# Score products of the next unit moved between two groups of transposes in the attention loop of a hybrid block

## The chip, the cores and the metric

The kernel runs on one core of one Trainium2 chip. The metric is the device time of one execution in microseconds; lower is better. A core has five engines that run at the same time: TensorE (matrix products; PE in the profile, with its weight loads shown apart as PEld), VectorE (DVE), ScalarE (ACT), GpSimd (POOL) and SyncE (SP), which here issues most of the transfers. TensorE writes its results to PSUM, a small memory of eight banks, from which VectorE or ScalarE must copy them before a bank can be used again.

## What is computed

The reference is a chain of four residual blocks over `x` of shape 4 x 256 x 512: an attention with rotary embedding, 32 heads of width 16 and an adapter prefix of 10 tokens; a gated linear layer; a state-space mixer on an inner width of 8192; and the same gated linear layer again. The change touches the attention alone:

```python
x = x + attn(_layernorm(x), ...)      # the change is in here
x = x + ffn(_layernorm(x), ...)
x = x + mixer(_layernorm(x), ...)
x = x + ffn(_layernorm(x), ...)

# attn, per batch b (4 of them), T = 256, 32 heads of width 16
q, k = rope(q), rope(k)
scores = einsum('bhqd,bhkd->bhqk', q, k) / sqrt(16)   # causal mask
y = einsum('bhqk,bhkd->bhqd', softmax(scores), v)
a = gating[0] * softmax(einsum('bhqd,xhkd->bhqk', q, ak) / sqrt(512))
y = y + einsum('bhqk,xhkd->bhqd', a, av)
return einsum('btc,oc->bto', y, w_proj)
```

## The kernel before

The attention is done in 32 units, unit `i` being four heads of batch `b = i // 8` (`u = i % 8`). A loop over `i` issues one pass for each unit; work of several units is in flight in each pass, one stage apart. In this loop the order of TensorE's instructions is exactly that of the program text (the loop stands in a manual schedule for TensorE), while VectorE, ScalarE and GpSimd get an order from the scheduler of the framework when the program is built. Every engine then runs its own instructions in that fixed order, and an instruction that has to wait holds up all that stand behind it on its engine. TensorE's instructions in pass `i` are, in this order:

- `scores(b, u)`: 16 products of queries and keys (`sc`, the code's line 492) into four banks of the pool `ps_s`, which only the scores use. The keys are needed a second time with neighbouring rows swapped; the swap is a pair of transfers on SP (`pc<-pc`, line 348) that follows ScalarE's copy of the transposed keys (`pc<-trp`, line 447).
- on even `u`, `adapter_scores`: products `pa` (line 457), which ScalarE copies out as `sa` (line 462);
- `pieces`: four transposes `trp` (line 444) of queries or keys for a later unit;
- a "long" step, where one is due: 12 products of 128x512 that make queries, keys, values or an output projection (`pq`, `po`, `pd`; lines 115 to 117);
- `weigh`: the values weighted by the exponentials of unit `i - 2` (`py`, lines 533 and 539);
- `turn`: 12 transposes of the exponentials of unit `i - 1` in three groups of four (`ptr`, line 523), each group into a bank of its own. ScalarE copies the first and third group, VectorE the second (`eT`, line 524);
- `gathered`: two transposes of the weighted values of unit `i - 3` (`try`, line 553), from which VectorE makes the reciprocal `ry` of the row sums and the result `y` (lines 558 and 559);
- on even `u`, the transposes `tra` (line 466) of the adapter scores, which ScalarE copies to `as` (line 467); and, in some passes, the transposes of a "turn" step: `tr` of a normalised tile (line 166), `try2` of finished results (line 610), `pt` of the adapter's weights (line 584).

All of these but `sc` and `py` take their banks from one pool, `ps` (tag `m`), which has three banks. Banks are given out when the program is built, and the first write into a bank waits for the last reader of what was in it before.

VectorE and ScalarE turn scores into exponentials. For each of the four heads VectorE adds the causal mask and takes the row maximum in one custom instruction (line 500, `e<-sc`, `nmx`): four over 256 columns and four over 128 columns. ScalarE then takes the exponentials (line 508), again four wide and four narrow ones. Unit `i`'s exponentials are needed by `turn` in pass `i + 1`.

`scores` is a generator, and where the pass resumes it decides what is issued there. Its steps in the kernel before: products and row maxima up to the first `yield`, wide exponentials up to the second, narrow ones up to the third. The pass used it so:

```python
scoring = scores(b, u)
next(scoring)          # products, row maxima
...                    # pa, trp
next(scoring)          # wide exponentials
...                    # long step, py, ptr
next(scoring)          # narrow exponentials
```

After the attention come the two gated layers and the mixer, whose products (lines 115 to 117, `pp`, `pog`, and line 1252) fill the rest of the time.

Of the kernel before, what the change touches and what calls it, by code (L numbers as in the profile page):

```python
# [79 lines left out]
def hybrid_kernel(  # L80
# [191 lines left out]
    def attention(later, region):  # L272
        with ExitStack() as es:
# [19 lines left out]
            def weights(w, src, tag, engine, pool=p2):  # L293
                for k in range(0, KC, 2):
                    r = pool.tile([P, 2, C], F32, name="ar", tag=tag)
                    if pool is p1:
                        load(r, src[:, k : k + 2, :])
                    for j in range(2):
                        if pool is not p1:
                            load(r[:, j, :], src[:, k + j, :])  # L300
                        split([v[:, k + j, :] for v in w], r[:, j, :], engine)
# [171 lines left out]
            def begin(b):  # L473
                state[b] = {
                    "as": p1.tile([P, 2, NH, NA], F32, name="as"),
                    "y": p1.tile([P, 2, C], F32, name="y"),
                    "ya": p1.tile([P, 2, C], F32, name="ya", tag="ya"),
                    "yT": [p1.tile([P, KC, L], F32R, name=f"yT{j}") for j in range(2)],
                }

            def scores(b, u):

                qT, kT = turned_[b, u // 2]
                es_ = [p2.tile([P, 4, (c + 1) * P], F32, name=f"e{c}", tag=f"e{c}") for c in range(2)]
                tops = {}
                banks_ = [ps_s.tile([P, 3, P], F32, name="sc", tag="sc") for _ in range(4)]
                for c, at in ((1, slice(0, 2)), (0, slice(2, 3))):
                    n = (c + 1) * P
                    for v in range(2):
                        for r in range(4):  # L490
                            rows = slice(32 * r, 32 * r + 32)
                            nc.tensor.matmul(
                                banks_[r][:, at, :].rearrange("p k i -> p (k i)"),
                                qT[rows, 0, u % 2, c * P : (c + 1) * P], kT[rows, v, u % 2, :n],
                                start=(v == 0), stop=(v == 1),
                            )
                for c, at in ((1, slice(0, 2)), (0, slice(2, 3))):
                    tops[c] = nm = p3.tile([P, 4], F32, name="nmx", tag="nmx", bufs=4)
                    for r in range(4):
                        nc.vector.tensor_tensor_reduce(  # L500
                            es_[c][:, r, :].rearrange("p (k i) -> p k i", i=P), banks_[r][:, at, :],
                            mask[:, 1 - c :, :], -1.0, 3e38, ALU.add, ALU.min, nm[:, r : r + 1],
                        )

                yield
                for c in (1, 0):
                    for r in range(4):
                        nc.scalar.activation(  # L508
                            es_[c][:, r, :], es_[c][:, r, :], AF.Exp, scale=-1.0, bias=tops[c][:, r : r + 1],
                        )  # L510
                    if c == 0:
                        all_es[8 * b + u] = es_
                    yield
# [31 lines left out]
            def taken(py):  # L545
                ys = p2.tile([P, L], F32, name="ys")
                nc.vector.tensor_copy(ys, py)
                return ys
# [87 lines left out]
            def fed(f, t):  # L636
                yield "turn", None
                xs = normed(f.norm, t)
                yield "long", max(0, B * 8 + t - 2)
                f.tile(t, xs, [ps.tile([P, FH], F32, name="pd", tag="m") for _ in range(2)])  # L640
# [35 lines left out]
            n = B * 8  # L676
# [5 lines left out]
            def moved(j, i):  # L682

                v = next(j, None)
                if v is None:
                    nexts.pop(j, None)
                else:
                    nexts[j] = v[0], i + 1 if v[1] is None else v[1]

            def step(stage, i):  # L690

                for j in [j for j, (s, r) in nexts.items() if s == stage and r <= i]:
                    moved(j, i)
# [15 lines left out]
            with tc.manual_schedule(engines={nc.tensor.engine}):  # L709
                for i in range(n):  # L710
                    b, u = divmod(i, 8)
                    if u == 0:
                        if i:
                            begin(b)
                        if b + 1 < B:
                            moved(prepared(b + 1), i)
                    scoring = scores(b, u)
                    next(scoring)
                    if i in FEEDS:
                        moved(fed(feed, FEEDS[i]), i - 1)  # L720
                    if i == 2:
                        nc.scalar.activation(a_s, a_s, AF.Exp)
                        nc.gpsimd.tensor_scalar(a_s, a_s, -1.0, None, ALU.mult)
                    if i == 3:
                        weights(wp_s, wproj, "ya", nc.gpsimd, p1)
                    if u % 2 == 0 and i > 0:
                        asides.append(adapter_scores(b, u // 2))
                        next(asides[-1])
                    if part:
                        next(part)  # L730
                    part = None
                    next(scoring)
                    step("long", i)
                    step("values", i)
                    if 2 <= i:
                        py = weigh(*divmod(i - 2, 8), eTs.pop(i - 2))
                    if 1 <= i:
                        eTs[i - 1] = turn(all_es.pop(i - 1))
                    next(scoring)
                    if 2 <= i:  # L740
                        yss[i - 2] = taken(py)
                    if 3 <= i:
                        gathered(*divmod(i - 3, 8), yss.pop(i - 3))
                    while asides:
                        next(asides.pop(0), 0)
                    step("turn", i)
                    if u == 7:
                        moved(adapted(b), i)
                    if 3 <= i:
                        if (i - 3) % 8 == 6:  # L750
                            moved(closed((i - 3) // 8, (0, 1, 2)), i)
                        if (i - 3) % 8 == 7:
                            moved(closed((i - 3) // 8, (3,)), i)

                    b, u = divmod(i + 3, 8)
                    if b < B:
                        part = pieces(b, u // 2, (i + 1) % 2)
                        next(part)
                    if i == 23:
                        inner.close()  # L760
                        feed = Feed("f", *(
                            later.enter_context(
                                tc.tile_pool(name=f"f{v}", bufs=v, side="right", reuse_waits="tile")
                            ) for v in (1, 2)
                        ))
                    if i in range(23, 27):
                        feed.weights(i - 23, nc.gpsimd)
                        feed.norm.stats(i - 23)
                    if i == 26:
                        feed.norm.root(0, 4)  # L770


                b = B - 1
                step("long", n)
                yss[n - 2] = taken(weigh(b, 6, eTs.pop(n - 2)))
                eTs[n - 1] = turn(all_es.pop(n - 1))
                gathered(b, 5, yss.pop(n - 3))
                step("turn", n)
                moved(fed(feed, 3), n - 1)
                step("turn", n)  # L780
                step("long", n + 1)
                step("values", n + 1)
                yss[n - 1] = taken(weigh(b, 7, eTs.pop(n - 1)))
                gathered(b, 6, yss.pop(n - 2))
                moved(closed(b, (0, 1, 2)), n)
                moved(fed(feed, 4), n)
                step("turn", n + 1)
                gathered(b, 7, yss.pop(n - 1))
                moved(closed(b, (3,)), n)
                step("long", n + 2)  # L790
                step("turn", n + 2)
                xs5 = normed(feed.norm, 5)
                assert not nexts, nexts
# [1118 lines left out]
```

## Time and profile before

| what | value |
|---|---|
| median of 3 runs | 1804.76 us (1802.36 to 1805.3) |
| profiled execution, its own time | 1805.61 us |
| its span | 1803.8 us |
| TensorE busy, weight loads | 1745.7 us (97%), 1417.8 us (79%) |
| VectorE, ScalarE, GpSimd busy | 1427.7 us, 1268.7 us, 240.9 us |
| mean granted TensorE clock | 0.989 |
| first and last score product | 31.7 us, 281.0 us from the span's start |
| first and last transpose of exponentials | 44.1 us, 298.0 us |

The profile is that of one execution. Its span runs from the first to the last instruction that it records; the execution's own time is 1.8 us longer. Busy times are sums over an engine's instructions. The ends of matmuls are modelled, so that PE shows as busy more than it works; starts of matmuls and of weight loads, and what a wait was ended by, are what the reading rests on. In a row of the timeline the columns are start and duration in microseconds, engine, code line, operation, output and inputs, sizes, how often, and in brackets the idle time before and what ended it.

### The profile page before, as it was taken

Reading aid. Unit: us, or ns where it says so; the run is one execution under the profiler, and the core shown is the slowest. Engines: PE = TensorE matmul, PEld = TensorE weight load, DVE = VectorE, ACT = ScalarE, POOL = GpSimd, SP = SyncE. Lnnn points to the kernel's source line nnn. Section 1 sums busy time; section 2 is a strip of 40 time slices with the busy share of each in tenths; the row PEclk is TensorE's granted clock in tenths of the full one; section 3 lists DMA queues with packets and bytes.
Section 4 is the critical chain, followed back from the end, with each engine's and each line's share of the span. In section 5 each row is a group of like instructions: output and inputs, shape, how many; then the busy total and the mean of one; then the engine's idle time right before and its main releaser. Section 6 shows DMA issues by size and latency. Waiting matters only on the chain.

```text
span 1803.8 us, 33220 instructions
## 1 busy us (share of the span) xinstructions
PE 1745.7 (97%) x12862; PEld 1417.8 (79%) x12862; DVE 1427.7 (79%) x2523; ACT 1268.7 (70%) x2293; POOL 240.9 (13%) x249
## 2 busy tenths in 40 slices
PE   7999988899999999999999999999999999999998
PEld 6777767778877888888888888888888888888877
DVE  5676676889998788787878797878788878887777
ACT  5676684578887668766866686668667867777754
POOL 5332320111110111011110101110111101101100
PEclk8999999999999999999999999999999999999999
DMA  4000100122344234423433252325333433343231
GB/s 157 19 19 19 47 26 26 43 71 99 109 127 137 80 106 154 120 85 99 153 100 100 88 162 90 109 81 176 103 94 112 135 106 94 115 138 115 85 97 56
DMA packets 136941, 173.71 MB, mean 96 GB/s; under 512 B 12752, under 2 KB 78032, under 8 KB 136784
## 3 DMA queue, kind: packets, MB, share of 16 engines
q1 hardware_dynamic: 127712, 138.57, 25.5%
q10 hardware_dynamic: 9072, 33.03, 4.8%
q8 instruction: 101, 1.65, 0.4%
q14 instruction: 56, 0.46, 0.1%
HBM read 131.71 MB, written 35.65 MB: 93 GB/s over the span
## 4 chain that ended last, share of the span: by engine, by line
PE 76%; DVE 11%; ACT 8%; issue 3%; DMA 1%; POOL 1%; SPq 0%; ACTq 0%; DVEq 0%; POOLq 0%
PE pp L115 13%; PE pp L117 12%; PE pp L116 12%; PE pyy L1252 7%; PE pog L115 6%; PE pog L117 6%; PE pog L116 6%; PE trx L1233 3%; DVE acc L980 2%; ACT e L508 1%; ACT em L1213 1%; DVE em L1226 1%; PE pq L115 1%; PE ptr L523 1%; PE pq L117 1%
## 5 line engine op out<-in xcount | busy, mean ns | idle before, releaser
L115 PE MATMUL pp<-mx,w 128*128 128x512 f32 x1144 | 459.3, 401 | 0.0
L117 PE MATMUL pp<-mx,w 128*128 128x512 f32 x1144 | 446.8, 391 | 0.0
L116 PE MATMUL pp<-mx,w 128*128 128x512 f32 x1144 | 446.1, 390 | 0.0
L1285 POOL TENSOR_TENSOR sq<-sq,x 128x1024 f32<-128x1024 f32 x54 | 132.1, 2446 | 1177.7 <-ACT x L1284 1177.7
L117 PEld LDWEIGHTS pp<-mx,w 128*128 128x128 f32 x1144 | 214.7, 188 | 46.2
L115 PEld LDWEIGHTS pp<-mx,w 128*128 128x128 f32 x1144 | 214.8, 188 | 44.7
L980 DVE SCALAR_TENSOR_TENSOR acc<-pp,cw_s,acc 128x1012 f32<-128x1012 f32 (+2 forms) x192 | 244.5, 1274 | 4.3
L116 PEld LDWEIGHTS pp<-mx,w 128*128 128x128 f32 x1144 | 215.1, 188 | 40.5
L1226 DVE TENSOR_TENSOR em<-em,gm 128x1280 f32<-128x1280 f32 x128 | 189.5, 1489 | 72.1 <-ACT em L1221 72.1
L115 PE MATMUL pog<-wo,gh 128*128 128x512 f32 x512 | 201.2, 393 | 2.0 <-DVE x L1381 2.0
L117 PE MATMUL pog<-wo,gh 128*128 128x512 f32 x512 | 200.2, 391 | 0.9 <-DVE gh L1364 0.9
L116 PE MATMUL pog<-wo,gh 128*128 128x512 f32 x512 | 199.8, 390 | 0.0
L1236 DVE TENSOR_TENSOR xd<-trx,dt_t 128x512 f32<-128x512 f32 x128 | 82.4, 685 | 141.5 <-PE trx L1233 141.5
L1152 ACT ACT_TABLE_LOAD x63 | 80.8, 1283 | 139.1 <-DVE acc L980 138.9
L1443 ACT ACTIVATE gt<-pp 128x1024 f32<-128x1024 f32 x64 | 65.6, 1025 | 145.0 <-PE pp L117 145.0
L1252 PEld LDWEIGHTS pyy<-em,xd 64*64 64x64 f32 x4096 | 130.2, 133 | 44.2 <-issue 17.6
L1213 ACT ACTIVATE em<-r,end_t 128x128 f32<-128x128 f32 x512 | 163.1, 389 | 0.8
L1252 PE MATMUL pyy<-em,xd 64*64 64x256 f32 (+3 forms) x4096 | 157.8, 300 | 3.1 <-DVE em L1226 3.0
L115 PEld LDWEIGHTS pog<-wo,gh 128*128 128x128 f32 x512 | 96.3, 188 | 24.8 <-issue 2.8
L508 ACT ACTIVATE e<-e,nmx 128x256 f32<-128x256 f32 (+1 forms) x256 | 97.2, 448 | 24.3 <-DVE nmx L500 24.2
L117 PEld LDWEIGHTS pog<-wo,gh 128*128 128x128 f32 x512 | 96.4, 188 | 22.3 <-DVE gh L1364 2.1
L116 PEld LDWEIGHTS pog<-wo,gh 128*128 128x128 f32 x512 | 96.4, 188 | 19.5
(324 smaller groups left out, 3094.5 us busy)
## 6 DMA issues: line engine op xcount, KB each, us to landing
wr<-in_win_dram SPq DMA_DIRECT2D x144, 256.0 KB, 2.7
r<-cumd SPq DMA_DIRECT2D x256, 128.0 KB, 2.9
spill<-gb ACTq DMA_DIRECT2D x63, 512.0 KB, 2.8
gr<-spill SPq DMA_DIRECT2D x120, 256.0 KB, 3.4
wor<-in_wout_dram SPq DMA_DIRECT2D x64, 256.0 KB, 4.4
pc<-pc SPq DMA_DIRECT2D x32, 128.0 KB, 2.0
out_dram<-x SPq DMA_DIRECT2D x7, 256.0 KB, 2.3
x<-in_x_dram SPq DMA_DIRECT2D x1, 1536.0 KB, 9.0
```

Source lines behind the costliest of these rows:

```text
L115: nc.tensor.matmul(o, lh, rh, start=(first and k == 0), stop=False)
L116: nc.tensor.matmul(o, lh, rl, start=False, stop=False)
L117: nc.tensor.matmul(o, ll, rh, start=False, stop=(last and k == n - 1))
L508: nc.scalar.activation(es_[c][:, r, :], es_[c][:, r, :], AF.Exp, scale=-1.0, bias=tops[c][:, r : r + 1],)
L980: nc.vector.scalar_tensor_tensor(av[:, :, d:], pv[:, :, : L - d], cw_s[:, ch, tap : tap + 1], av[:, :, d:], ALU.mult, ALU.add,)
L1152: nc.scalar.activation(pair(x2).rearrange("p k u i -> p u k i"), acc.rearrange("p (u k i) -> p u k i", u=2, i=Q), AF.Silu,)
L1213: nc.scalar.activation(piece(e, j, c, 2 - c, 2), rv[:, j, 2:, :], AF.Exp, bias=end_t[:, 2 * j + c, h : h + 1],)
L1226: nc.vector.tensor_tensor(e, e, gm, ALU.mult)
L1236: nc.vector.tensor_tensor(xd[:, hs, :].rearrange("p c (h d) -> p c h d", h=2), tr.rearrange("p c (h d) -> p c h d", h=2), dt_t[:, hs, 2 * ...
L1252: nc.tensor.matmul(py[d, u, j * L + c * Q : (j + 1) * L].rearrange("p (k i) -> p k i", i=Q), xd[us, 4 * j + c, d], piece(es2[hh], j, c)[us ...
L1285: (nc.gpsimd if n < NB - 2 else nc.vector).tensor_tensor(sqs[g], sqs[g], x2, ALU.add)
L1443: nc.scalar.activation(gts[i], pp, AF.Silu)
```

## The change

A fourth stop is put into `scores`, between the products and the row maxima. The loop now makes the generator of the next unit at the end of the transposes of exponentials, after the copy `taken` and before `gathered`, and runs it to this first stop, so that TensorE's order becomes `ptr`, `sc` of unit `i + 1`, `try`, `tra` and so on. In the next pass the generator is taken up where it stands, and its row maxima are issued in the text where they were before. Only the first unit's products are still issued at the head of its pass.

```diff
@@ scores
                                 qT[rows, 0, u % 2, c * P : (c + 1) * P], kT[rows, v, u % 2, :n],
                                 start=(v == 0), stop=(v == 1),
                             )
+                yield
                 for c, at in ((1, slice(0, 2)), (0, slice(2, 3))):
                     tops[c] = nm = p3.tile([P, 4], F32, name="nmx", tag="nmx", bufs=4)
@@ head of a pass
-                    scoring = scores(b, u)
+                    if not i:
+                        ahead = scores(0, 0)
+                        next(ahead)
+                    scoring = ahead
                     next(scoring)
@@ after turn
                     next(scoring)
                     if 2 <= i:
                         yss[i - 2] = taken(py)
+                    if i + 1 < n:
+                        ahead = scores(*divmod(i + 1, 8))
+                        next(ahead)
                     if 3 <= i:
                         gathered(*divmod(i - 3, 8), yss.pop(i - 3))
```

## Prediction

> **What bounds the kernel.** I read the page first: its busy times, and the chain of work that ended last.
>
> ```profile
> PE 1745.7 (97%) x12862; PEld 1417.8 (79%) x12862; DVE 1427.7 (79%) x2523; ACT 1268.7 (70%) x2293; POOL 240.9 (13%) x249
> ...
> PE 76%; DVE 11%; ACT 8%; issue 3%; DMA 1%; POOL 1%; SPq 0%; ACTq 0%; DVEq 0%; POOLq 0%
> ```
>
> TensorE carries the chain, before and after the attention, so a microsecond that it loses or gains in the attention passes to the end. Next, busy time in stretches of the attention (columns: length, busy time of PE, PEld, DVE, ACT, POOL with counts, granted clock, DMA share, GB/s):
>
> ```profile
> 233.50:252.30 18.80, 16.92 (x205) 13.05 (x198) 13.49 (x66) 17.13 (x46) 4.54 (x14) 0.99 0.05 16
> 97.00:114.00 17.00, 14.55 (x147) 11.56 (x146) 11.37 (x48) 14.57 (x37) 4.30 (x11) 1.00 0.09 32
> ...
> 115.00:161.00 46.00, 45.26 (x398) 34.80 (x398) 33.48 (x144) 29.59 (x73) 13.48 (x29) 1.00 0.04 13
> ...
> 230.50:234.00 3.50, 3.50 (x41) 2.87 (x40) 2.83 (x19) 3.44 (x6) 3.50 (x6) 0.54 0.00 0
> ```
>
> Passes with a long step run on TensorE (45.26 of 46.00); passes without one (7, 8, 15, 16, 23 to 26) run on ScalarE (17.13 of 18.80). What TensorE waits for, from 44 to 300 us (total, times, longest):
>
> ```profile
> PE try L553 <- ACT eT L524: 5.0, 7, 2.2
> ...
> PE pt L584 <- ACT eT L524: 1.4, 3, 0.6
> PE ptr L523 <- ACT av L431: 1.3, 1, 1.3
> ```
>
> These are bank waits: `ptr` fills all three banks of `ps`, and the next transpose waits for a copy. Score products use other banks and can fill this gap. With the smaller rows of the same kind (0.2 to 0.8 each), waits on `eT` make some 9 us, the most that filling it can bring. Last, pass 12 in the timeline:
>
> ```profile
> 138.19 1.53 PE L523 MATMUL ptr<-con,e 128*128 128x128 f32 x12
> ...
> 140.07 0.20 PEld L466 LDWEIGHTS tra<-con,sa 80*128 80x128 f32 x2 [0.29 <-DVE eT L524]
> ...
> 140.36 0.69 PE L492 MATMUL sc<-pc,pc 32*128 32x256 f32 x16
> 140.47 0.29 ACT L467 COPY as<-tra 128x160 f32<-128x160 f32 x1
> ...
> 141.06 0.42 DVE L500 CUSTOM_DVE_ANT_0 e<-sc,acon 128x256 f32<-128x256 f32 x1 [0.48 <-PE sc L492]
> ...
> 141.35 0.47 PE L115 MATMUL pq<-wv,axs 128*128 128x512 f32 x1
> ...
> 141.59 0.91 ACT L508 ACTIVATE e<-e,nmx 128x256 f32<-128x256 f32 x2 [0.84 <-DVE nmx L500]
> ```
>
> `tra` waits 0.29 us for a bank; the copy `as` and, on VectorE, `y` are done before the row maxima and exponentials begin, and `pq` starts 3.16 us after `ptr`. Below, P is the start of a pass's first `ptr`.
>
> **What the change moves.** No instruction is added or removed. I compared the order of both built programs on each engine, and the bank and wait of each TensorE instruction in them. SP's order is the same, so no transfer is moved; on GpSimd only the adapter's `as<-as,anm` falls behind two pieces of stacking, in three passes. The large change is on the two engines that the scheduler orders. As `sc` is now early, three row maxima stand before `ry` and a fourth before `y`; and on ScalarE two wide exponentials now stand before `as`, three before `sa`. Banks moved as well: `pq`, which waited for VectorE's `y` in most passes, now takes the bank of `tra` (even passes) or `pa` (odd passes) and so waits for `as` or `sa`. What was done early and cheaply is put behind ScalarE's exponentials, and TensorE's long step stands behind that.
>
> *An even pass.* The weight loads of `ptr` take 1.29 us, and a 0.17 us gap stands before `sc` in the timeline: `sc` starts at P+1.46. The first row maximum came 0.70 to 0.82 us after `sc` where VectorE was free: P+2.2. The first exponential comes 0.53 later (141.06 to 141.59): P+2.7. Wide exponentials follow each other by 0.41 (two from 141.59, the next copy at 142.41): `as` starts at 3.52, takes 0.29, and 0.06 passes before TensorE goes on: `pq` at P+3.87 instead of P+3.16. That is 0.71 lost. TensorE itself arrives at about P+3.0, as the waits on `eT` go, so the gain of 0.2 to 0.3 is inside this number. Six such passes (4, 6, 12, 14, 20, 22): 4.3 us.
>
> *An odd pass.* Three exponentials, then `sa` (0.35): 3.93 + 0.35 + 0.06 = P+4.34, against P+3.19 (145.10 to 148.29). 1.15 lost, in passes 3, 5, 13, 21: 4.6 us.
>
> *Passes with more transposes.* `y` ends at 2.2 + 3 x 0.345 + 0.24 + 0.345 + 0.29 = P+4.12. Passes 11 and 19: `trp` waits for that; `sa` stands behind a cast of 0.37 and three exponentials, so `pq` is at P+4.7 instead of 3.69: 2.0 us. Passes 9 and 17: the cast of `axs` (0.59) stands before `sa`, P+4.9 instead of 4.3 (119.23 less 114.91): 1.2. Passes 10 and 18: three casts of 0.37 are now strewn among the exponentials, and `pq` needs the second difference on VectorE, P+5.45 instead of 4.03: 2.8. Together 14.9 us.
>
> *The other passes*, with bounds from the nearest waits. Pass 1: `sc` must wait for the swap of `pc`, which ScalarE finished at 45.62 and which lands some 2.0 to 2.7 us later, while TensorE is ready at 46.4; the adapter's `tra`, queued behind, start 1.5 us later and VectorE's row maxima come between their operands, but the 1.1 us of `sc` no longer follow. 0 to 2.5, I take 1.3. Passes 7 and 8, 15 and 16: the wait of 1.3 on `av` goes, since exponentials no longer pile up before it; in exchange `tr` and its `axs` stand behind five exponentials, about 1.5 later. Between -1.5 and +2.0 for each pair; 0.8 each, 1.7 in all. Passes 23 to 26 run on ScalarE, which gets its exponentials sooner; the waits there were 2.2, 0.5 and 0.3 on TensorE and 1.6 on ScalarE. Between -5 and 0; -3. Passes 27 and 28: the swap's landing ended a wait of 0.5 of `sc` already; the products are now wanted 1.4 us sooner, and 28 is an even pass. 0 to 3; 1.9. Passes 29 to 31: waits on `fe` and `fx` (1.0 and 1.8) get shorter. -3 to +1; -1.5.
>
> Sum: 14.9 + 1.3 + 1.7 - 3 + 1.9 - 1.5 = 15.3 us. On the profiled execution's 1805.6 us this gives 1820.9; the median of the runs is 0.85 lower, so 1820.
>
> [...] The new pauses recur each pass. In the trace, pauses do not slow the clock while they are short: from 97 to 114 us TensorE was idle for 2.45 of 17 us and the granted clock was 1.00; only after the 2.2 us wait did it fall, to 0.54. I therefore add nothing. [...]
>
> **Rivals.** *Faster:* the ScalarE-bound passes decide. If exponentials that start 0.9 us sooner remove the waits on `eT`, `av` and `pt` (5.0 + 1.4 + 1.3) and the copies `as` and `sa` still come in time, the kernel gains up to 8 us: 1797. For it speaks that these waits are there; against it that `as` would have to end before P+3.1, so that the first row maximum had to start by P+1.5, when `sc` has only begun. 0.08. *No change:* the pauses cost half (7.5 us), as the next `ptr` was waiting for exponentials anyway and now is not, and ScalarE's passes give 8 back. Against: `ptr` waited 0.20 us on `e` eleven times, no more than the 0.20 us that it shows with no releaser. 1802 to 1808, at 1805; 0.08. *Much slower:* where `sc` is wanted before its swap has landed in every second pass, not in three, the wait of 1.7 us that I count in pass 27 comes in 12 passes: 20 us more, 1840. Against: in pass 12 `pc` is copied by P+4.4 and lands by P+7.1, and `sc` needs it at P+9. 0.09. My forecast: 0.75.
>
> **Range and chances.** Low end of the sum: `sc` and row maxima 0.17 sooner in 16 passes (-2.7), passes 23 to 31 at their best (-4), pass 1 free (-1.3): 1812; taking in half of "no change" it reaches 1807. High end: the upper bounds of all the other passes (+11): 1832. Differences below 0.2% can't be told from none here. Faster 0.08, same 0.08, slower 0.84.
>
> **What would show it.** Right: in the trace after, `pq <- ACT as` and `pq <- ACT sa` are TensorE's largest waits, some 0.7 to 1.2 us in each long pass; `try` and `tra` no longer wait on `eT`; three rows of line 500 stand before `ry`; passes 23 to 27 are shorter by some 3 us; the clock stays at 1.00. Wrong: `pq` starts at P+3.2 or sooner, or the row maxima do not start before P+2.5, or the clock falls between 60 and 220 us.

## The result and the profile after

| | median, us | lowest to highest | runs |
|---|---|---|---|
| before | 1805.03 | 1802.36 to 1805.36 | 4 |
| after | 1820.78 | 1818.68 to 1821.96 | 4 |

The changed kernel takes 1.0084 of the time before, with a 95% interval of 1.0067 to 1.0102: 0.8% slower. Its profiled execution took 1818.68 us and its span is 1816.9, against 1805.61 and 1803.8 before. The last `ptr` of the loop starts 13.74 us later (310.46 against 296.72) and the whole span is 13.1 us longer, so the difference is made inside the attention loop and carried to the end.

First the page, busy times and the chain of work that ended last. As predicted, no engine has more work; TensorE's share of the chain grows from 76% to 82%.

```profile
PE 1743.0 (96%) x12862; PEld 1415.0 (78%) x12862; DVE 1421.6 (78%) x2523; ACT 1268.8 (70%) x2293; POOL 241.0 (13%) x249
...
PE 82%; DVE 8%; ACT 6%; issue 2%; DMA 1%; POOL 1%; SPq 0%; ACTq 0%; DVEq 0%; POOLq 0%
```

Next the stretches: passes 9 to 14, which were TensorE's own (45.26 busy in the 46.00 us that the prediction shows; the six passes took 46.91), and a long stretch that covers most of the loop (columns as before: length, busy time of PE, PEld, DVE, ACT, POOL with counts, granted clock, DMA share, GB/s). TensorE now stands still for 6.1 of 52.45 us in the first and 21.45 of 182 us in the second, and the granted clock is 1.00 in both.

```profile
120.40:172.85 52.45, 46.32 (x418) 35.51 (x414) 32.82 (x144) 31.98 (x80) 13.68 (x29) 1.00 0.04 16
60.00:242.00 182.00, 160.55 (x1463) 123.45 (x1461) 113.96 (x499) 114.67 (x285) 53.38 (x105) 1.00 0.07 23
```

What TensorE waits for, from 44 to 315 us (total, times, longest). Before, the largest row was `try` on `eT` with 5.0 us. That row is gone: the products fill the gap, as the change says. In its place stand the small copies `as` and `sa` of ScalarE, and `y` of VectorE.

```profile
PE pq L115 <- ACT sa L462: 5.0, 6, 1.1
PE trp L444 <- DVE y L560: 3.9, 5, 0.9
PE pq L115 <- ACT as L467: 3.6, 4, 0.9
PE sc L492 <- DMA pc<-pc: 3.2, 3, 1.7
PE try L611 <- ACT as L467: 2.8, 3, 1.0
```

Last, pass 12 in the timeline, which now begins at P = 146.64:

```profile
148.10 0.68 PE L492 MATMUL sc<-pc,pc 32*128 32x256 f32 x16
...
148.81 0.42 DVE L501 CUSTOM_DVE_ANT_0 e<-sc,acon 128x256 f32<-128x256 f32 x1 [0.35 <-PE sc L492]
148.99 0.30 PE L466 MATMUL tra<-con,sa 80*128 80x80 f32 x2
...
149.34 0.91 ACT L509 ACTIVATE e<-e,nmx 128x256 f32<-128x256 f32 x2 [0.49 <-DVE nmx L501]
...
149.85 0.20 DVE L559 RECIPROCAL ry<-try 128x8 f32<-128x8 f32 x1
...
150.16 0.27 ACT L467 COPY as<-tra 128x160 f32<-128x160 f32 x1
...
150.27 0.28 DVE L560 TENSOR_TENSOR y<-try,ry 128x128 f32<-128x128 f32 x1
...
150.48 0.50 PE L115 MATMUL pq<-wv,axs 128*128 128x512 f32 x1 [0.88 <-ACT as L467]
```

`tra` starts at once and ends by 149.3, but its copy `as` begins only at 150.16, behind two exponentials on ScalarE. On VectorE three row maxima stand ahead of `ry` and a fourth ahead of `y`. `pq`, which takes `tra`'s bank, waits 0.88 us for the copy. The pass takes 7.62 us against 6.91.

### The profile page after: what moved, and what is told of

The parts are those of the page before. It is cut to its first block, busy times and chain, and to the rows that moved or that the text cites. A ratio compares the mean times of both kernels' runs of the same rounds, so it can differ in the third digit from the quotient of the medians.

```text
span 1816.9 us, 33215 instructions
## 1 busy us (share of the span) xinstructions
PE 1743.0 (96%) x12862; PEld 1415.0 (78%) x12862; DVE 1421.6 (78%) x2523; ACT 1268.8 (70%) x2293; POOL 241.0 (13%) x249
## 4 chain that ended last, share of the span: by engine, by line
PE 82%; DVE 8%; ACT 6%; issue 2%; DMA 1%; POOL 1%; SPq 0%; ACTq 0%; DVEq 0%; POOLq 0%
PE pp L115 14%; PE pp L117 13%; PE pp L116 13%; PE pyy L1259 7%; PE pog L115 6%; PE pog L116 6%; PE pog L117 6%; PE trx L1240 3%; PE ptr L524 2%; ACT e L509 2%; DVE acc L987 1%; PE pq L115 1%; PE pq L117 1%; PE pq L116 1%; DVE e L501 1%
## 5 line engine op out<-in xcount | busy, mean ns | idle before, releaser
L509 ACT ACTIVATE e<-e,nmx 128x256 f32<-128x256 f32 (+1 forms) x256 | 99.7, 453 | 16.2 <-DVE nmx L501 16.1
```

Source lines behind the costliest of these rows:

```text
L509: nc.scalar.activation(es_[c][:, r, :], es_[c][:, r, :], AF.Exp, scale=-1.0, bias=tops[c][:, r : r + 1],)
```

## The experiments

Ratios are to the kernel before, measured beside the kernels of the experiment; its median was 1805.8 to 1806.6 us there. The theory is that the loss is made by the order of work on ScalarE and VectorE (exponentials and row maxima ahead of the copies that free TensorE's banks), and that the early products themselves gain. The rival is that the products cost by their place on TensorE.

### Both halves of the queue order held

`issue_after` queues what is issued in its block behind a named instruction of the same engine, by order alone, with no wait for that one to end. `held["y"]` is the last `y`, `held["a"]` the last copy `as` or `sa`. TensorE's order stays that of the change.

```diff
+            def behind(k):
+                return tc.issue_after(held[k]) if k in held else ExitStack()
...
-                nc.scalar.copy(sa, pa)
+                held["a"] = nc.scalar.copy(sa, pa).ins
...                                     (the same for `as`, and held["y"] for `y`)
+                        with behind("y"):
                             nc.vector.tensor_tensor_reduce(
...
+                        with behind("a"):
                             nc.scalar.activation(
```

> The products stay where the change puts them on TensorE, but on VectorE the row maxima of the next unit are queued behind `y`, and on ScalarE its exponentials behind `as` and `sa`, as they stood before. If the order on these two engines is what the change costs: `pq` starts at about P+3.2 to P+3.5 in the passes with a long step, the rows `pq <- ACT as` and `pq <- ACT sa` (8.6 us together after the change) fall below 2 us, and the time is 1801 to 1808 us, 13 to 19 below the changed kernel. If instead the early products themselves cost, by the banks that the other tiles then get or by keeping `try` and `tra` later on TensorE: 1814 us or more, and the waits turn up on another releaser.

Then each half alone: `h_dve` has only `behind("y")`, `h_act` only `behind("a")`.

> Only the row maxima are held behind `y`; the exponentials stand where the scheduler puts them, in some even passes one of them still ahead of `as`, while `sa` is ahead of all. If both queues share the cost by the steps of the prediction (copies behind two or three exponentials of 0.41 us): one exponential is left in some six passes, 6 x 0.4 = 2.5 us, so 1804 to 1810 us. If the cost sits on ScalarE's queue alone and VectorE's order does not matter, this kernel is as good as the one with both held only because its exponentials are later too; if the early products themselves cost: 1814 us or more.

> Only the exponentials are held behind `as` and `sa`; three to four row maxima still stand ahead of `ry` and `y` on VectorE. If the copies behind exponentials are the whole cost: 1801 to 1808 us. If the late `y` is a cost of its own (`trp` waited 3.9 us for it after the change, `pt` 1.6): 1808 to 1814 us, with `trp <- DVE y` the largest row left. If the early products themselves cost: 1814 us or more.

| row maxima behind `y` | exponentials behind `as`, `sa` | median, us | ratio, 95% interval |
|---|---|---|---|
| no (the change) | no | 1820.8 | 1.0084 [1.0067, 1.0102] |
| no | yes (`h_act`) | 1804.6 | 0.9996 [0.9987, 1.0005] |
| yes (`h_dve`) | no | 1800.7 | 0.9976 [0.9967, 0.9985] |
| yes | yes (`h_both`) | 1799.8 | 0.9967 [0.9954, 0.998] |

With both held the change is not a loss but a gain of 6 us, with the products in the same place on TensorE; that is 1.2 us below the range that I gave. Pass 12 of that run (P = 139.49) shows it:

```profile
140.96 0.68 PE L497 MATMUL sc<-pc,pc 32*128 32x256 f32 x16
...
142.18 0.29 ACT L467 COPY as<-tra 128x160 f32<-128x160 f32 x1 [0.48 <-PE tra L466]
142.28 0.29 DVE L567 TENSOR_TENSOR y<-try,ry 128x128 f32<-128x128 f32 x1
...
142.49 0.41 DVE L507 CUSTOM_DVE_ANT_0 e<-sc,acon 128x256 f32<-128x256 f32 x1
142.53 0.19 PEld L115 LDWEIGHTS pq<-wv,axs 128*128 128x128 f32 x1 [0.22 <-ACT as L467]
...
143.01 0.91 ACT L516 ACTIVATE e<-e,nmx 128x256 f32<-128x256 f32 x2
```

`pq` still takes `tra`'s bank and still has `as` as its releaser, but `as` comes as soon as `tra` is there: `pq` starts at P+3.04, where before it was P+3.16 and after the change P+3.84. So in this pass the choice of banks costs nothing by itself; it only decides who waits for a late copy. The exponentials begin at P+3.52, no sooner than before (P+3.40), and the pass is still the shorter one, 6.82 us against 6.91, since the products fill the gap.

The waits of TensorE that the view lists from 44 to 315 us, summed by releaser:

| waits of TensorE on | before | after | `h_act` | `h_both` |
|---|---|---|---|---|
| copies `as` and `sa` | 0 | 18.4 | 3.7 | 1.8 |
| `y` | 0.9 | 6.5 | 6.7 | 1.7 |
| ScalarE's copies `eT` | 7.4 | 1.5 | 1.9 | 1.9 |

The times follow the rows. From the change to `h_act` the waits on copies fall by 14.7 us and the median by 16.2. From `h_act` to `h_both` the waits on `y` fall by 5.0 and the median by 4.8. `h_act`'s time lies in the range of "the copies are the whole cost" (1801 to 1808 us), and the copies are most of it; but a late `y` costs on its own as well, about 5 us, as its rows and the step to `h_both` show, so that range was set too wide to tell the two apart. In `h_dve` holding the row maxima is almost enough, since an exponential can't start before its row maximum. It came out below the 1804 to 1810 that I expected: for some six passes with one exponential left ahead of `as` I had counted 2.5 us, but the trace has four such passes (2, 8, 16 and 24), and `h_dve` takes 0.9 us more than `h_both`, which itself is below its range.

### Is it the holding that gains?

The control: TensorE's order of before (no early products), and both queues held, with the casts `axs` and `yT` as well (the next but one experiment).

```diff
-                    if i + 1 < n:
+                    if i + 1 in EARLY:          # EARLY = (): no unit
                         ahead = scores(*divmod(i + 1, 8))
                         next(ahead)
```

A unit that is not in EARLY has its products where they were before the change.

> The control for the holding: TensorE's order is that of before, with no products early, and row maxima and exponentials are held behind `y`, `as`, `sa` and the casts as in the fastest run. Before the change most of them stood that way already; what the holding alters is that `sa` comes ahead of two exponentials in odd passes. If the gain of the held kernels over before is that of the early products (6 us at the change's own place, 10 us behind `try` with units 1 and 2 left out): 1803 to 1807 us, no difference from before. If it is the holding itself that gains: 1796 to 1801 us.

1806.6 us, ratio 1.0005 [0.9997, 1.0014]: no difference from before. The gain of the held kernels belongs to the early products. Which of them make it is the next question.

### Early products at the end of the loop alone

`late29` has EARLY = 29 to 31, `late31` has unit 31 only; nothing is held in either.

> The products are early for units 29, 30 and 31 alone; in all other passes the order is that of before. In the changed kernel the passes 28 to 31 were 4.6 us shorter than before (+0.5, +1.3, -1.1, -5.3). If that gain belongs to the early products of these units: 1799 to 1803 us, 2 to 6 below before. If it came only from the delay that the earlier passes had piled up (the adapter's chain and the feed's loads being ready sooner, as seen from there): 1804 to 1807 us, no gain.

> Only unit 31 has its products early, nothing is held. In the run with units 29 to 31 early pass 28 lost 0.5, 29 lost 1.3, 30 gained 1.1 and 31 gained 5.3 us. If the gain is that the row maxima of unit 31 no longer stand behind the adapter's chain of the last batch on VectorE and ScalarE (`anm`, `as`, `asum`), it belongs to this unit alone: 1798.5 to 1801 us. If units 29 and 30 have to be early for it: 1803 to 1806 us.

1801.4 us, ratio 0.9979 [0.997, 0.9988], and 1801.6 us, 0.9976 [0.9966, 0.9986]; the second is 0.6 us above its range and well below its rival's. Passes 28 to 31 of `late29` repeat the changed kernel's differences within 0.02 us (+0.50, +1.33, -1.14, -5.34), though nothing is delayed ahead of them: a pass's gain or loss is its own. And unit 31 alone brings the gain: pass 31 takes 11.39 us before and 6.05 in `late31`. Its cause stands in pass 31's timeline. Before, the products of unit 31 ran at 280.55, and their row maxima came 3.71 us later, behind the adapter's sums on VectorE; `fx`, for which the next `ptr` waits, stands behind the row maxima:

```profile
283.52 0.82 DVE L574 TENSOR_REDUCE asum<-as 128x64 f32<-128x640 f32 x1 [1.36 <-ACT as L572]
284.26 0.41 DVE L500 CUSTOM_DVE_ANT_0 e<-sc,acon 128x256 f32<-128x256 f32 x1
...
284.71 2.87 ACT L508 ACTIVATE e<-e,nmx 128x256 f32<-128x256 f32 x8 [1.23 <-DVE nmx L500]
...
287.08 0.45 DVE L248 TENSOR_TENSOR fx<-pd,fb 128x288 f32<-128x288 f32 x1
...
287.58 0.42 PEld L523 LDWEIGHTS ptr<-con,e 128*128 128x128 f32 x4 [1.83 <-DVE fx L248]
...
290.43 0.61 PE L115 MATMUL pd<-fw,axs 128*128 128x288 f32 x1 [0.40 <-DVE eT L524]
...
295.93 0.64 PE L533 MATMUL py<-eT,av 128*32 128x256 f32 x8
```

With unit 31 early they come ahead of the adapter's chain, and the next `ptr` runs all 12 transposes without a pause:

```profile
278.01 0.68 PE L492 MATMUL sc<-pc,pc 32*128 32x256 f32 x16
...
279.14 0.41 DVE L501 CUSTOM_DVE_ANT_0 e<-sc,acon 128x256 f32<-128x256 f32 x1
...
284.97 1.53 PE L524 MATMUL ptr<-con,e 128*128 128x128 f32 x12
...
286.84 0.40 PE L115 MATMUL pd<-fw,axs 128*128 128x288 f32 x1
...
290.23 0.64 PE L534 MATMUL py<-eT,av 128*32 128x256 f32 x8
```

The waits are only part of these 5.3 us. From the first `ptr` to the first `pd`, where the waits are, before took 5.10 us and `late31` 1.87: 3.2 us. From the first `pd` to `py`, 24 products `pd`, before took 5.50 us and `late31` 3.39: the other 2.1 us. They are the same products, but before most of them ran at a granted clock of 0.50. The first row is of before, just after the wait on `fx`, the second is pass 31 of `late31`:

```profile
288.40:295.20 6.80, 6.29 (x26) 5.92 (x27) 3.96 (x13) 0.99 (x3) 0.73 (x1) 0.50 0.00 0
```

```profile
284.97:291.02 6.05, 5.94 (x58) 5.14 (x54) 5.37 (x19) 2.19 (x5) 1.64 (x2) 1.00 0.00 0
```

The trace of `held_only`, which has the order of before on TensorE, shows the low clock at this place too (its `pd` load their weights every 0.24 us, as those of before do at 0.50; those of `late31`, at 1.00, every 0.13); the changed kernel, at 1.00 in its pass 31, does not.

The same order on VectorE that costs in a plain pass gains here, since what is pushed back, `anm` and `asum`, has nobody waiting for it yet.

### Products one group of transposes later

The products stand between `try` and the adapter's `tra`; nothing is held.

```diff
-                    if i + 1 < n:
-                        ahead = scores(*divmod(i + 1, 8))
-                        next(ahead)
                     if 3 <= i:
                         gathered(*divmod(i - 3, 8), yss.pop(i - 3))
+                    if i + 1 < n:
+                        ahead = scores(*divmod(i + 1, 8))
+                        next(ahead)
                     while asides:
```

> Nothing is held, but the products of the next unit stand behind `try`, between `try` and the adapter's `tra`. In the built program `ry` and `y` then stand ahead of the row maxima again, `sa` behind two exponentials as before the change, and `as` behind one exponential (0.41 us) where the change has two. If the loss is exponentials and row maxima in front of the copies: an even pass keeps some 0.3 of its 0.71 us, an odd one nothing, and the late passes keep their gain: 1799 to 1806 us, though only two transposes have changed places with the products. If the products cost by standing anywhere ahead of `tra` and the long step: 1812 us or more.

1813.0 us, ratio 1.0039 [1.0024, 1.0053], its runs spread from 1806.9 to 1818.3: the forecast of 1799 to 1806 missed, and the number is the rival's. By passes, the theory holds in the plain ones: the even plain passes take 6.62 to 6.64 us (before 6.90 to 6.98), the odd plain ones what they took before. The largest losses stand elsewhere: passes 8 to 11 lose 4.2 us and 16 to 19 lose 4.3. These are the passes with casts of more transposes (`axs`, `yT`), and in the built program exponentials and row maxima still stood ahead of those. Pass 8 in the timeline shows five exponentials, then the copy `paT` for which TensorE's next transposes wait:

```profile
108.02 2.00 ACT L509 ACTIVATE e<-e,nmx 128x128 f32<-128x128 f32 x5
...
109.93 0.56 ACT L589 COPY paT<-pt 80x512 f32<-80x512 f32 x1
...
110.55 0.66 PE L166 MATMUL tr<-con,axn 128*128 128x128 f32 x4 [1.22 <-ACT paT L589]
```

Not all of the loss is in the loop. Of the 6.8 us by which this profile's span is longer than that of before, 2.8 stand ahead of the last `ptr` and 4.0 behind it. There a projection `po` waits 1.76 us for the difference `axs`, a wait that before does not have, and the granted clock is 0.50 for 6.8 us from 337.3, for 3.4 us at the like place of before.

Whether exponentials and row maxima ahead of the casts are the cause was the next question: hold the casts too.

### The casts held as well

`split` writes `axs0` and `yT0` on ScalarE and the differences `axs1` and `yT1` on VectorE; in the attention's transposes it now also sets what is held:

```diff
-        nc.scalar.copy(hl[0], v)
-        engine.tensor_tensor(hl[1], v, hl[0].bitcast(F32), ALU.subtract)
+        high = nc.scalar.copy(hl[0], v)
+        low = engine.tensor_tensor(hl[1], v, hl[0].bitcast(F32), ALU.subtract)
+        if hold:
+            held["a"], held["y"] = high.ins, low.ins
```

`t_all` has this with the products behind `try`, `c_all` with the products where the change puts them.

> The products stand behind `try` as in the run that only moved them there (1813.0 us), all units, but row maxima are now held behind `y` and behind the differences `axs1` and `yT1`, and exponentials behind `as`, `sa` and the casts `axs0` and `yT0`. In the run without holding, the passes without such casts were as short as before the change or shorter (6.63 against 6.91 in pass 12), and passes 8 to 11 and 16 to 19, which have them, lost 8.5 us together. If row maxima and exponentials in front of these casts are the cause, these passes come back: 1797 to 1803 us. If TensorE's own order is the cause (products ahead of `tra` in passes with many transposes): 1807 us or more.

> The products stand where the change puts them, all units; held are both queues with the casts too. Against the run that held only `y`, `as` and `sa` (1799.8 us) passes 8, 10, 16 and 18 had lost 1.5 us together with exponentials or row maxima strewn among the casts. If these 1.5 us are the casts': 1797.5 to 1799.5 us. If they are time that the passes 7 and 15 gained and gave back: 1799 to 1801 us, no difference.

`t_all`: 1799.4 us, ratio 0.9962 [0.9948, 0.9976]; with TensorE's order unchanged, the 14 us between it and `p_try` (0.77% by the ratios) come from the two queues. The wait of `po` on `axs` is gone too. Passes 8 to 11 fall from 38.9 to 35.1 us and 16 to 19 from 39.0 to 35.2 (before 34.7 for both). `p_try`'s miss was mine in listing only `as`, `sa` and `y` as what the exponentials must not pass.

`c_all`: 1799.4 us, ratio 0.9969 [0.9957, 0.998], no difference from `h_both`. The time lies in both of its ranges, so the passes have to decide. Passes 8, 10, 16 and 18 are as long as there (11.77, 8.18, 11.79, 8.18): their losses against before were not the casts'.

### Leaving units out

Ahead of pass 2, `sc` waits 1.7 us for its swap when units 1 and 2 are early.

`best`: as `h_both`, with EARLY = 3 to 31. `best2`: without 9, 11, 17, 19, 25 and 30 as well. `t_3`: as `t_all`, with EARLY = 3 to 31.

> Both queues held as in the run that held row maxima and exponentials (1799.8 us), but the products of units 1 and 2 stay where they were before the change; early are those of units 3 to 31. With all units early the second pass ended 2.95 us later than before the change (65.57 against 62.62 us from the start of the span), as the products of units 1 and 2 wait for a swap of `pc` that lands late. If that is the price of these two units alone: 1796 to 1798 us. If it is the holding that delays the start: 1799 to 1801 us.

> As the run that leaves out units 1 and 2, and without units 9, 11, 17, 19, 25 and 30 too, whose passes (8, 10, 16, 18, 24, 29) were 0.3 to 1.4 us longer than before the change in the run that held both queues (0.33 + 0.40 + 0.36 + 0.38 + 1.36 + 0.99 = 3.8 us). If these losses belong to the pass in which the products are early: 1793 to 1795 us. If they are time that the pass ahead of them gained and that ScalarE's work takes back (pass 23 gained 1.9, 24 lost 1.4; passes 30 and 31 gained 6.3 after 29 lost 1.0), leaving these units out brings nothing or loses: 1797 to 1801 us.

> As the run with products behind `try` and all held, but the products of units 1 and 2 stay where they were before the change. The wait of 1.7 us of `sc` for its swap in the second pass and what follows it go: 1 to 2.5 us less than that run, 1795 to 1799 us. If the start varies by as much from run to run whatever the kernel, as the profiles suggest (the first `ptr` at 42.1 to 46.0 us): no difference.

| | median, us | ratio, 95% interval |
|---|---|---|
| `best` | 1797.4 | 0.9952 [0.994, 0.9963] |
| `best2` | 1796.4 | 0.9952 [0.994, 0.9964] |
| `t_3` | 1795.4 | 0.9945 [0.993, 0.9959] |

Leaving out units 1 and 2 is within its forecast in `best` (2.3 us below `h_both`, though the intervals overlap). `t_3` is within its 1795 to 1799 us, but 4.0 us below `t_all`, where 1 to 2.5 were expected; these intervals overlap too, so the size of this step stays uncertain. In the profiles the last `ptr` of `t_3` comes 4.8 us sooner than that of `t_all`: 1.9 by the start ahead of the first `ptr`, 1.9 by pass 1, and 1.0 by passes 24 and 25, where the mean granted clock of pass 24 was 0.84 in `t_all` and 1.00 in `t_3`. The wait for the swap is gone in `best` and `t_3`. Leaving out the other six brings nothing that can be told; `best2`'s 1796.4 lies between its two ranges. By passes, 10 and 18 return to 7.76 and 7.79 us as soon as units 11 and 19 are not early, so those 0.4 us belong to the early products; pass 8 stays at 11.78, so there the 0.3 us are not unit 9's; I take them to be paid back from the 1.3 us that pass 7 gained.

`t_3` is the fastest kernel of this study: 0.55% less than before, and it beats both kernels. Set beside `late31`, which has one unit early, holds nothing and already gains 0.24%, the other early units bring 0.1 to 0.3%: the intervals of `best` and `t_3` lie below that of `late31`, those of `h_both` and `t_all` overlap it.

## Why the prediction was right

The forecast was 1820 us, slower, and the main loss came for the reason that it gave. The steps:

- **An even plain pass**: `pq` predicted at P+3.87, measured at P+3.84 in pass 12; six passes predicted at 4.3 us, measured at 4.37 from the starts of `ptr`.
- **An odd plain pass**: P+4.34 predicted. In pass 13 (P = 154.26) `sa` runs for 0.35 us from 158.22, behind three exponentials, and `pq` starts at 158.62, which is P+4.36. Four passes: 4.6 predicted, 4.81 measured.
- **Passes with more transposes**: 14.9 us with the above predicted, 14.84 measured (11 and 19: 1.84 for 2.0; 9 and 17: 1.33 for 1.2; 10 and 18: 2.49 for 2.8).
- **Passes 7, 8, 15 and 16**: 1.3 for 1.7. The wait on `av` went and pass 7 gained 0.86, but pass 15 lost 0.30 and passes 8 and 16 lost 0.92 and 0.94. **Passes 27 and 28**: 1.27 for 1.9. **Pass 1**: 1.5 for 1.3, a profile of one execution, as its start varies.
- **Passes 23 to 26: mis-sized**, -0.1 for -3. Pass 23 gained 3.81 and pass 24 lost 3.12. The step that failed is "ScalarE gets its exponentials sooner", priced from the waits of TensorE. Its own busy time leaves less than that. Over these four passes, before and with both queues held:

```profile
225.19:252.24 27.05, 22.23 (x247) 17.00 (x243) 19.36 (x84) 25.32 (x62) 9.46 (x20) 0.94 0.08 27
```

```profile
225.84:252.31 26.47, 22.11 (x246) 17.17 (x242) 18.45 (x82) 25.34 (x61) 10.25 (x19) 0.94 0.07 27
```

ScalarE had 1.73 us to spare, so no order could gain 3 while all its work stays in these passes. With the queue order put right 0.6 came. The change itself gained 0.7 in passes 23 and 24 together, since most of what pass 23 saved moved into pass 24, where ScalarE was busy for 10.01 of 10.64 us (7.43 of 7.54 before) and `trp` waits 1.2 us for `paT`. It lost 0.6 again in passes 25 and 26, where `try` waits 0.84 us for `as`, and the granted clock was 0.77 from 253.00 to 260.50. `t_3` takes 25.03 us for the four passes, but with only 23.09 us of ScalarE's work left in them.

- **Passes 29 to 31: mis-sized**, -5.14 for -1.5, outside its bounds of -3 to +1. I priced the waits on `fe` and `fx` that TensorE showed and did not look at where the row maxima of unit 31 stood: 3.71 us after their products, behind `asum`. `late31` shows that this is the gain, and its trace that 3.2 of the 5.3 us of pass 31 stand ahead of `pd`, where the waits are, and 2.1 in the products `pd`, most of which before ran at a granted clock of 0.50. The prediction put the clock at nothing, for it read that the clock fell "only after the 2.2 us wait"; in the trace of before it fell again at 288.4, after the wait of 1.60 us on `fx`.

The two mis-sized terms nearly cancel (+2.9 and -3.6), so that the sum of 15.3 us met the measured 13.7 in the loop by luck better than its parts deserve. The interval of the ratio, 1.0067 to 1.0102, is 12 to 18 us. The range does not follow from the prediction's own bounds: passes 23 to 31 at their best are 5.4 us below the sum, not 4, and the upper bounds of the other passes add 10.1, not 11; the result lies inside either way. Of the signs that it named, one did not come: passes 23 to 27 are 0.7 us longer, not 3 shorter.

**The rivals.** *Faster* failed on its condition. It asked that the copies `as` and `sa` still come in time and gave 1797 us; the kernels whose row maxima are held, and with them the exponentials, meet that condition by force and take 1795.4 to 1800.7. That its price fits is in part luck: it was made of the waits on `eT`, `av` and `pt`, but in `h_both` passes 29 to 31 gain 5.3 us, passes 2 to 28 only 3.3, and pass 2 begins 2.95 us later. *Much slower* did not come: `sc` waited for its swap three times, 3.2 us in all, not every second pass. *No change* failed as the pauses cost their full length.

**The clock.** TensorE was idle for 12% of the 182 us shown above, in pauses of up to 1.3 us in nearly every pass, and was granted 1.00 throughout. Outside that stretch it was 0.50 at times in both kernels, as in pass 31 of before, above, and from 256.90 to 260.30 after the change. That the clock fell "only after the 2.2 us wait" does not hold: in before it also fell at 49.4 us, where no wait of the 5 us ahead was over 0.87 us, and after the change at 256.9, where none was over 1.21. These traces give no length of a single wait that decides it; adding nothing to the sum was right for the 182 us.

## What to carry to other kernels

Where only one engine's order is fixed by hand, moving an instruction on it moves the work that depends on it on the scheduled engines too: look at the built order of every engine, and ask which short copies that free a bank now stand behind long work that has become ready sooner. If the move is right and the order is what costs, pin that order: here a few lines of ordering turned a loss of 0.8% into a gain of 0.3%, and with two units left out and the products one group later it is 0.55%. Price a stage by the busy time of the engine that fills it, not by the waits that others show there; read the granted clock behind a long wait, since what a removed wait is worth can be more than its length (in pass 31, 3.2 us where the waits are and 2.1 us of products, most of which ran at 0.50 before); and look up what stands between a result and its first reader.

## What the runs showed of the hardware that was not expected

- The start of the loop differs between profiles: the first `ptr` of pass 1 began at 41.9 to 46.0 us, at 44.02 in before, 45.55 in `held_only`, whose order in the loop is nearly the same, and 42.1 in `late31`, which differs from before in unit 31 alone. Passes of equal order in the middle of the loop repeat within a few hundredths (pass 12: 6.91, 6.91 and 6.90 us in before, `held_only` and `late29`). I take the start to vary by execution, which the spread of before's runs (1801.6 to 1809.6 us) allows, but no kernel was profiled twice to show it.
- The swap's landing differs too: between 245 and 270 us `sc` waited 1.4 us for it in `best` and 0.4 in `h_both`, which differ in units 1 and 2 alone.
